# A selective scan's products partly a chunk earlier, and a layer norm pass in written order

## The chip, the core and the metric

The kernel runs on one core of one Trainium2 chip. The metric is the device time of one execution in microseconds (us). A profiled execution was also taken; its trace gives the start and length of every instruction on TensorE (PE, with its weight loads PEld), VectorE (DVE), ScalarE (ACT) and GpSimd (POOL), and the waits between them. SP is the queue from which nearly all DMAs are issued.

## The reference

Two layers act on x, 256 x 256 positions with 128 channels, all in float32. Layer 0 is a group norm, a layer norm, and attention along each row with a bias from the pairs. Layer 1 is a group norm, a 3 x 3 depthwise convolution and a selective scan in four directions. What bears on the change, cut to its core:

```python
# layer 0, on the group-normed input
x = (x - mu) * rsqrt(var + EPS) * gamma + beta        # layer norm over the channels
pair_bias = x @ Wb                                    # 4 heads
...
# layer 1, for each of K = 4 directions over L = 65536 positions, 256 channels, 16 states
delta = softplus(dts + dt_bias)
def step(h, inp):
    d_t, x_t, B_t, C_t = inp
    dA = exp(d_t[..., None] * As)
    h = dA * h + (d_t * x_t)[..., None] * B_t[:, :, None, :]
    y = einsum('bkdn,bkn->bkd', h, C_t)
    return (h, y)
...                                                    # the four directions' y summed
y = (y - mu) / sqrt(var + 1e-05) * ln_w + ln_b
y = y.reshape(b, h, w, d) * z
return y @ w_out.T
```

## The kernel before

It has these stages, one after the other: the first group norm's statistics; the layer norm's pass; the attention; the convolution; the scan. The change touches the second and the last.

**The layer norm's pass** (L165 to L227) goes over 32 blocks of 2048 positions, each held as 16 slices of 128 positions by 128 channels. A block is loaded (xb, L173), GpSimd subtracts the group means (xg, L177), VectorE multiplies by the group factors, which lie in PSUM (L180), and takes each slice's mean and variance (L186, L188; into mv). GpSimd makes rs, the inverse root of the variance, by an addition and a power (L36, L37). VectorE makes nb, the mean times -rs (L192). Even slices are then normalized on VectorE with a tensor_scalar (L203), odd ones on ScalarE (L195). TensorE transposes four slices at a time into a PSUM tile tp (L216), ScalarE evacuates it into xT (L220), TensorE multiplies xT by Wb (L224), and ScalarE evacuates this into pb (L225). Both go to DRAM. The pools hold three buffers of each SBUF tile. The order of instructions on each engine is not as written there: the framework's scheduler sets it.

**The scan** (from L1042) has its order written by hand. There are 512 chunks of 512 positions: 128 for each direction, the directions one after the other. A chunk q has eight groups g of 32 channels by 16 states, laid on 128 partitions as four state quarters, and a group takes four scans, n = 0 to 3. For each of these ScalarE makes dA by an exponential (L1081; dAl in SBUF for n = 0, dA in PSUM with three buffers for the others), and VectorE scans (L1107). VectorE also makes the additive terms of three scans in one product (L838). The terms of the fourth come another way. In "products" ScalarE multiplies the transposed delta times x (duT) by B (tiles bt, L797, 16 instructions for each half of a chunk; half h has groups 4h to 4h+3, and one buffer bt for each half), and TensorE transposes a group's part back into bl (L809). GpSimd multiplies the states by C (L1127), TensorE sums these over the states (L853).

Other work of ScalarE's, TensorE's and GpSimd's is cut into pieces by generators, of which each of the 32 places of a chunk, (g, n), takes one. A list "counts" says how many products a place takes:

```python
counts = {1: [0, 2, 3, 3], 3: [2, 2, 2, 2], 5: [0, 0, 2, 2], 6: [1, 1, 2, 2], 7: [2, 2, 2, 0]}
            if g == 5 and n == 2 and q + 1 < NQ:
                multiplying.append(products(q + 1, 0))
            if g == 1 and n == 1:
                multiplying.append(products(q, 1))
```

"prepare" (L684) makes a later chunk's operands; it begins at group 5 and goes on into group 2 of the next chunk: two copies xs in group 6, the product pb in group 7, its evacuation bc (L710) at group 7, n = 2, then two Abs and two Relu, an exponential (L736), two shifts (L748, L751), and at group 2, n = 0, a logarithm (L758), which needs another table on ScalarE. "turn" (L769) transposes delta times x at group 4. When a half is summed, "evacuate" copies it (yo, L1026). At the end of a chunk of the first three directions, "store" adds the y of the direction before and writes it out. In the last direction "finish" (L910) does so and then takes the layer norm: ScalarE copies ys, VectorE takes the statistics, GpSimd makes rs and nb, ScalarE makes four yn (L952), TensorE transposes them, ScalarE makes gz (L971), GpSimd multiplies by z (L976), TensorE multiplies by w_out, and ScalarE evacuates xo (L995). The generator counts its places from group 3, n = 0, of the next chunk, and "until(now, then)" lets then - now places pass. So 16 is group 7, n = 0, and 23 is group 0, n = 3.

Of the kernel before, what the change touches and what calls it, by code (L numbers as in the profile page):

```python
# [8 lines left out]
F32 = mybir.dt.float32  # L9
# [7 lines left out]
P = 128  # L17
# [16 lines left out]
def rsqrt(nc, out, v, eps, neg_half):  # L34

    nc.gpsimd.tensor_scalar(out, v, eps, None, ALU.add)  # L36
    nc.gpsimd.tensor_tensor(out, out, neg_half.to_broadcast(list(out.shape)), ALU.pow)  # L37
# [29 lines left out]
def attention_and_scan_kernel(  # L67
# [97 lines left out]
    with tc.tile_pool(name="ln", bufs=3) as ln, tc.tile_pool(  # L165
        name="lnps", bufs=3, space=PSUM
    ) as lnps, tc.tile_pool(name="r1ps", bufs=1, space=PSUM) as r1ps:

        r1_p = r1ps.tile([P, D], F32, name="r1_p")
        nc.vector.tensor_copy(r1_p, r1)  # L170
        for b in range(S // RB):
            xb = ln.tile([P, NSL, D], F32, name="xb")
            nc.sync.dma_start(  # L173
                xb, x[b * BT : (b + 1) * BT, :].rearrange("(s p) c -> p s c", p=P)
            )
            xg = ln.tile([P, NSL, D], F32, name="xg")
            nc.gpsimd.tensor_tensor(  # L177
                xg, xb, m1.unsqueeze(1).to_broadcast([P, NSL, D]), ALU.subtract
            )
            nc.vector.tensor_tensor(  # L180
                xg, xg, r1_p.unsqueeze(1).to_broadcast([P, NSL, D]), ALU.mult
            )
            st = ln.tile([P, NSL, 6], F32, name="st")
            mv = ln.tile([P, NSL, 2], F32, name="mv")
            for s in range(NSL):
                nc.vector.bn_stats(st[:, s, :], xg[:, s, :])  # L186
            for s in range(NSL):
                nc.vector.bn_aggr(mv[:, s, :], st[:, s, :])  # L188
            rs = ln.tile([P, NSL], F32, name="rs")
            rsqrt(nc, rs, mv[:, :, 1], 1e-5, neg_half)  # L190
            nb = ln.tile([P, NSL], F32, name="nb")
            nc.vector.scalar_tensor_tensor(nb, mv[:, :, 0], -1.0, rs, ALU.mult, ALU.mult)  # L192
            for s in range(NSL):
                if s % 2:
                    nc.scalar.activation(  # L195
                        xg[:, s, :],
                        xg[:, s, :],
                        AF.Identity,
                        bias=nb[:, s : s + 1],
                        scale=rs[:, s : s + 1],  # L200
                    )
                else:
                    nc.vector.tensor_scalar(  # L203
                        xg[:, s, :],
                        xg[:, s, :],
                        mv[:, s, 0:1],
                        rs[:, s : s + 1],
                        ALU.subtract,
                        ALU.mult,
                    )  # L210
            xT = ln.tile([D, BT], F32, name="xT")
            pb = ln.tile([H, BT], F32, name="pb")
            for q in range(NSL // 4):
                tp = lnps.tile([D, 512], F32, name="tp")
                for j in range(4):
                    nc.tensor.transpose(  # L216
                        tp[:, j * P : (j + 1) * P], xg[:, 4 * q + j, :], ident
                    )
                cols = slice(q * 512, (q + 1) * 512)
                nc.scalar.activation(  # L220
                    xT[:, cols], tp, AF.Identity, bias=beta_s, scale=gamma_s
                )
                pp = lnps.tile([H, 512], F32, name="pp")
                nc.tensor.matmul(pp, wb_s, xT[:, cols], start=True, stop=True)  # L224
                nc.scalar.copy(pb[:, cols], pp)  # L225
            nc.sync.dma_start(xT_d[:, b * BT : (b + 1) * BT], xT)
            nc.sync.dma_start(pb_d[:, b * BT : (b + 1) * BT], pb)  # L227


    with tc.tile_pool(name="abias", bufs=1) as ab:  # L230
# [448 lines left out]
    def until(now, then):  # L679

        for _ in range(then - now):
            yield
# [227 lines left out]
    def finish(q, yos):  # L910

        a = steps[q][1]
        yl = summed.pop(q)
        yield
        sums_ = []
        for g in range(2):
            ps = sps.tile([P, 2, DI], F32, name="ysum", tag="mm")
            add_sum(  # L920
                ps,
                yl[:, 2 * g : 2 * g + 2, :],
                [
                    (ps[:, j, h * P : (h + 1) * P], yos[h][:, (2 * g + j) * P : (2 * g + j + 1) * P])
                    for j in range(2)
                    for h in range(2)
                ],
            )
            sums_.append(ps)
            yield  # L930
        yield
        ys = io.tile([P, 4, DI], F32, name="ys", tag="yt", bufs=1)
        for g, ps in enumerate(sums_):
            nc.scalar.copy(ys[:, 2 * g : 2 * g + 2, :], ps)
            yield
        zt = io.tile([P, 2, T], F32, name="zl", bufs=1)
        nc.sync.dma_start(zt, z_d[:, a : a + T].rearrange("(h p) t -> p h t", p=P))
        st = io.tile([P, 4, 6], F32, name="yst")
        mv = io.tile([P, 4, 2], F32, name="ymv")
        rs = io.tile([P, 4], F32, name="yrs")  # L940
        nb = io.tile([P, 4], F32, name="ynb")
        for j in range(4):
            nc.vector.bn_stats(st[:, j, :], ys[:, j, :])
        for j in range(4):
            nc.vector.bn_aggr(mv[:, j, :], st[:, j, :])
        rsqrt(nc, rs, mv[:, :, 1], 1e-5, neg_half)
        nc.gpsimd.tensor_tensor(nb, mv[:, :, 0], rs, ALU.mult)
        nc.gpsimd.tensor_scalar(nb, nb, -1.0, None, ALU.mult)
        yield from until(6, 16)
        yn = io.tile([P, 4, DI], F32, name="yn", tag="yl", bufs=1)  # L950
        for j, now, then in ((0, 16, 19), (1, 19, 20), (2, 20, 23), (3, 23, 27)):
            nc.scalar.activation(  # L952
                yn[:, j, :],
                ys[:, j, :],
                AF.Identity,
                bias=nb[:, j : j + 1],
                scale=rs[:, j : j + 1],
            )
            yield from until(now, then)
        tps = []  # L960
        for h in range(2):
            tp = sps.tile([P, T], F32, name="tpz", tag="mm")
            for j in range(4):
                nc.tensor.transpose(
                    tp[:, j * P : (j + 1) * P], yn[:, j, h * P : (h + 1) * P], ident
                )
            tps.append(tp)
        yield from until(27, 30)
        gz = io.tile([P, 2, T], F32, name="gz", bufs=1)
        for h, tp in enumerate(tps):  # L970
            nc.scalar.activation(  # L971
                gz[:, h, :], tp, AF.Identity, bias=lnb_s[:, h : h + 1], scale=lnw_s[:, h : h + 1]
            )
            yield
        yield from until(32, 36)
        nc.gpsimd.tensor_tensor(gz, gz, zt, ALU.mult)  # L976
        yield from until(36, 40)
        xr = io.tile([P, 4, D], F32, name="xr", bufs=1)
        nc.sync.dma_start(xr, x2_d[a : a + T, :].rearrange("(j p) c -> p j c", p=P))
        yield from until(40, 55)  # L980
        po = sps.tile([P, 4, D], F32, name="po", tag="mm")
        nc.tensor.matmul(po, ident, xr, start=True, stop=True)
        for j in range(4):
            for h in range(2):
                nc.tensor.matmul(
                    po[:, j, :],
                    gz[:, h, j * P : (j + 1) * P],
                    wout_s[:, h, :],
                    start=False,
                    stop=True,  # L990
                    skip_group_check=True,
                )
        yield from until(55, 58)
        xo = io.tile([P, 4, D], F32, name="xo", tag="xr", bufs=1)
        nc.scalar.copy(xo, po)  # L995
        nc.sync.dma_start(out[a : a + T, :].rearrange("(j p) c -> p j c", p=P), xo)
# [60 lines left out]
    begin_sums(0, 0)  # L1057
    turning, multiplying, summing = [], [], []
    bls = {(0, 0): turn_back(0, 0)}

    counts = {1: [0, 2, 3, 3], 3: [2, 2, 2, 2], 5: [0, 0, 2, 2], 6: [1, 1, 2, 2], 7: [2, 2, 2, 0]}
    for s, (q, g) in enumerate(all_steps):
        k, a = steps[q]
        nxt = all_steps[s + 1] if s + 1 < len(all_steps) else None
# [11 lines left out]
        for n, i in enumerate((NB, *range(NB))):  # L1076
# [18 lines left out]
                turning.append(turn(q + 1))  # L1095
            if g == 5 and n == 2 and q + 1 < NQ:
                multiplying.append(products(q + 1, 0))
            if g == 1 and n == 1:
                multiplying.append(products(q, 1))
            if g == 5 and n == 1 and q + 2 < NQ:  # L1100
                preparing.append(prepare(q + 2))
            piece(turning)
# [90 lines left out]
```

## Time and profile before

| | |
|---|---|
| median of 3 runs | 32542.47 us (32539.59 to 32545.17) |
| profiled execution | 32538.74 us, span 32537.0 us |
| VectorE busy | 29634.3 us (91%) |
| GpSimd busy | 25719.5 us (79%) |
| ScalarE busy | 25277.6 us (78%) |
| TensorE matmuls | 24581.2 us (76%) |
| layer norm's pass | 112.9 to 615.2 us |
| scan | 5714 to 32485 us |

A profile row of a group gives line, engine, operation and tiles (written <- read), shape, count, then busy time and the mean of one in ns, then the idle time of the engine ahead of these and what ended it. A row of the waits gives who waited for whom, the total in us, how often, and the longest. A row of the timeline gives start, length, engine, line, operation, tiles, shape and count, and in brackets the idle time ahead and who ended it.

### The profile page before, as it was taken

How to read it: one execution, taken by the hardware profiler on the slowest of the kernel's cores; microseconds unless marked ns; L12 is line 12 of the kernel's file. 1: busy time of each engine (PE TensorE's matmuls, PEld its weight loads, DVE VectorE, ACT ScalarE, POOL GpSimd, SP SyncE). 2: the span in 40 equal slices, each digit the busy share in tenths (PEclk: the TensorE clock that was granted, in tenths of full speed). 3: DMA queues.
4: the chain of work that ended last, by engine and by line, in shares of the span. 5: the costliest groups of instructions: out<-in, count | busy, mean ns of one | idle time of the engine just before them, and what ended most of it. 6: DMA issues, size and time to landing. Idle time of an engine off the chain costs nothing.

```text
span 32537.0 us, 380541 instructions
## 1 busy us (share of the span) xinstructions
PE 24581.2 (76%) x122902; PEld 11561.7 (36%) x122902; DVE 29634.3 (91%) x28991; ACT 25277.6 (78%) x50438; POOL 25719.5 (79%) x11291
## 2 busy tenths in 40 slices
PE   5999989777777777777777777777777777777777
PEld 2555544223222223333333333333333333333333
DVE  7666643999999999999999999999999999999999
ACT  4555522888888888888888888888888888888887
POOL 3222200899999999999999999999999999999998
PEclk8999999777777777777777777777777777777777
DMA  3001023444444444444444444444444455554554
GB/s 137 29 28 30 28 93 123 110 108 109 110 109 108 108 109 119 118 118 119 120 120 118 117 119 121 119 119 118 120 120 118 118 123 123 122 121 121 122 122 112
DMA packets 2100469, 3518.55 MB, mean 108 GB/s; under 512 B 201112, under 2 KB 1187096, under 8 KB 2022560
## 3 DMA queue, kind: packets, MB, share of 16 engines
q1 hardware_dynamic: 2093296, 3476.09, 42.8%
q8 instruction: 967, 15.84, 0.2%
q10 hardware_dynamic: 5168, 18.12, 0.1%
q14 instruction: 1038, 8.50, 0.1%
HBM read 2754.18 MB, written 739.25 MB: 107 GB/s over the span
## 4 chain that ended last, share of the span: by engine, by line
DVE 31%; PE 27%; ACT 26%; issue 10%; POOL 5%; DMA 1%; DVEq 0%; SPq 0%; POOLq 0%; ACTq 0%
DVE bx L1107 17%; DVE bx L838 9%; PE yp L853 7%; ACT dA L1081 6%; PE ur L827 5%; ACT bt L797 4%; POOL bx L1127 2%; ACT dAl L1081 2%; PE pc L526 2%; ACT L758 2%; ACT L1081 2%; PE av L356 2%; POOL at L333 2%; ACT du L751 2%; PE atp L345 2%
## 5 line engine op out<-in xcount | busy, mean ns | idle before, releaser
L1127 POOL TENSOR_TENSOR bx<-bx,C_r 128x2048 f32<-128x2048 f32 x4096 | 18604.5, 4542 | 334.5 <-POOL hst L1126 6.0
L1107 DVE TENSOR_TENSOR_SCAN bx<-dA,hst,bx 128x512 f32<-128x512 f32 x12192 | 15061.1, 1262 | 455.3 <-ACT dA L1081 455.3
L1081 ACT ACTIVATE dA<-dr,A_s 128x512 f32<-128x512 f32 x12288 | 8345.5, 684 | 2974.6 <-DVE bx L1107 2865.2
L827 PE MATMUL ur<-du,spread 128*128 128x512 f32 x8192 | 5998.0, 823 | 4593.9 <-DVE bx L838 4544.3
L838 DVE TENSOR_TENSOR bx<-B_r,ur 128x1536 f32<-128x1536 f32 x4096 | 7067.5, 1725 | 39.1 <-DMA dr<-de_d 39.1
L797 ACT ACTIVATE bt<-duT,B_t 128x128 f32<-128x128 f32 x16384 | 5625.5, 394 | 0.0
L1107 DVE TENSOR_TENSOR_SCAN bx<-dAl,hst,bl 128x512 f32<-128x512 f32 x4064 | 5091.9, 1253 | 5.3 <-PE bl L809 4.3
L853 PE MATMUL yp<-bx,gather 128*32 128x512 f32 x32768 | 4808.1, 739 | 7.4 <-POOL bx L1127 6.4
L809 PE MATMUL bl<-ident,bt 128*128 128x128 f32 x16384 | 2817.3, 297 | 2060.9 <-DVE bx L1107 2049.9
L827 PEld LDWEIGHTS ur<-du,spread 128*128 128x128 f32 x8192 | 1519.7, 232 | 5194.1 <-DVE bx L838 5178.5
L809 PEld LDWEIGHTS bl<-ident,bt 128*128 128x128 f32 x16384 | 1871.7, 148 | 3949.2 <-DVE bx L1107 2874.1
L333 POOL TENSOR_TENSOR at<-at,sm 128x2048 f32<-128x2048 f32 x256 | 922.3, 3603 | 2708.9 <-DVE sm L332 2595.6
L1081 ACT ACTIVATE dAl<-dr,A_s 128x512 f32<-128x512 f32 x4096 | 2915.1, 712 | 0.0
L853 PEld LDWEIGHTS yp<-bx,gather 128*32 128x32 f32 x32768 | 1110.2, 134 | 4153.9 <-issue 4018.1
L1126 POOL COPY hst<-bx 128x4 f32<-128x4 f32 x4096 | 773.6, 189 | 1830.0 <-DVE bx L1107 1800.0
L325 ACT ACTIVATE at<-at,mx 128x256 f32<-128x256 f32 x2048 | 1016.1, 498 | 472.3 <-DVE mx L321 467.9
L755 POOL TENSOR_TENSOR e<-e,du 128x1024 f32<-128x1024 f32 x512 | 1206.6, 2357 | 137.7 <-DMA C_r<-bc_d 137.7
L766 POOL TENSOR_TENSOR du<-delta,xs 128x1024 f32<-128x1024 f32 x512 | 1208.9, 2361 | 40.2
L762 POOL TENSOR_TENSOR delta<-delta,lg 128x1024 f32<-128x1024 f32 x512 | 1208.8, 2361 | 40.2
L721 PE MATMUL pv<-bc,dtw_s 8*128 8x512 f32 x2048 | 1014.3, 614 | 256.8 <-ACT bc L710 256.8
L760 POOL TENSOR_TENSOR lg<-lg,e 128x1024 f32<-128x1024 f32 x512 | 1204.9, 2353 | 0.2 <-ACT lg L758 0.2
L354 DVE COPY aT<-atp 128x512 f32<-128x512 f32 x512 | 353.5, 690 | 772.8 <-PE atp L345 772.8
(172 smaller groups left out, 33209.5 us busy)
## 6 DMA issues: line engine op xcount, KB each, us to landing
dr<-de_d SPq DMA_DIRECT2D x4096, 256.0 KB
C_r<-bc_d SPq DMA_DIRECT2D x2048, 256.0 KB
B_r<-bc_d SPq DMA_DIRECT2D x2048, 192.0 KB
de_d<-delta SPq DMA_DIRECT2D x512, 512.0 KB
xtok<-xc_d SPq DMA_DIRECT2D x256, 512.0 KB
xtok<-xc_d SPq DMA_DIRECT2D x512, 256.0 KB
yl<-y_d SPq DMA_DIRECT2D x512, 256.0 KB
y_d<-yt SPq DMA_DIRECT2D x512, 256.0 KB
```

Of the source, the lines that this page charges most:

```text
L333: nc.gpsimd.tensor_tensor(at, at, sm.unsqueeze(3).to_broadcast([P, H, 2, S]), ALU.mult,)
L755: nc.gpsimd.tensor_tensor(e, e, du, ALU.subtract)
L762: nc.gpsimd.tensor_tensor(delta, delta, lg, ALU.add)
L766: nc.gpsimd.tensor_tensor(du, delta, xs, ALU.mult)
L797: nc.scalar.mul(bt[:, b, :, j, :], duT[:, b, h * P : (h + 1) * P].rearrange("t (g c) -> t g c", c=32), B_t[:, b, n : n + 1],)
L809: nc.tensor.transpose(bl[:, b * P : (b + 1) * P], bt[:, b, g % 4].rearrange("t j c -> t (j c)"), ident)
L827: nc.tensor.matmul(ur, spread[:, g % 4].rearrange("p j c -> p (j c)"), prepared[q][2][:, g // 4, :], start=True, stop=True,)
L838: nc.vector.tensor_tensor(bx[:, :NB, :], prepared[q][3], ur.unsqueeze(1).to_broadcast([P, NB, T]), ALU.mult,)
L853: nc.tensor.matmul(yp[32 * g : 32 * g + 32, :], gather, hc[:, i, :], start=(i == 0 and steps[q][0] != ORDER[0]), stop=True, skip_group_che ...
L1081: nc.scalar.activation(dA, dr, AF.Exp, scale=A_s[:, k, g // 4, g % 4, i : i + 1])
L1107: nc.vector.tensor_tensor_scan(hs[:, i, :], dA, hs[:, i, :] if i < NB else bls.pop((q, g)), 0.0 if a == 0 else hst[:, g, i : i + 1], ALU.mult,
L1127: nc.gpsimd.tensor_tensor(hs, hs, prepared[q][4], ALU.mult)
```

## The change

In the scan, the products of a chunk's second half are queued at group 7 of the chunk before rather than at group 1 of their own, and the counts put four of the 16 there, four in group 1 and eight in group 3. The first half's are put closer together. Ahead of the loop the first chunk's first four are made. In "finish" the four yn stand one place or more earlier and the two gz one place later.

In the layer norm's pass the order is written by hand. Loads run two blocks ahead, the subtraction one block ahead, and a block is normalized after the statistics and rsqrt of the next one have been issued. The means are copied to a PSUM tile mp, from which nb reads them. The product with Wb and its evacuation come one group of four slices behind the transposes.

```diff
+        def token_stats(xg):
...
+            mp = r1ps.tile([P, NSL], F32, name="mp", bufs=2)
+            nc.vector.tensor_copy(mp, mv[:, :, 0])
+            return mv, mp
+
+        def normalize(b, xg, mv, mp, rs):
...
-            nc.vector.scalar_tensor_tensor(nb, mv[:, :, 0], -1.0, rs, ALU.mult, ALU.mult)
+            nc.vector.scalar_tensor_tensor(nb, mp, -1.0, rs, ALU.mult, ALU.mult)
...
+            for q in range(NQ0 + 1):
+                if q < NQ0:
+                    tps[q] = lnps.tile([D, 512], F32, name="tp")
...
+                if q:
+                    cols = slice((q - 1) * 512, q * 512)
+                    pp = lnps.tile([H, 512], F32, name="pp", bufs=2)
+                    nc.tensor.matmul(pp, wb_s, xT[:, cols], start=True, stop=True)
+                    nc.scalar.copy(pb[:, cols], pp)
...
+        with tc.manual_schedule():
+            xbs = {b: load_block(b) for b in range(2)}
+            xg = center(xbs.pop(0))
+            before = None
+            for b in range(NB0):
+                if b + 2 < NB0:
+                    xbs[b + 2] = load_block(b + 2)
+                nxt_xg = center(xbs.pop(b + 1)) if b + 1 < NB0 else None
+                mv, mp = token_stats(xg)
+                rs = ln.tile([P, NSL], F32, name="rs")
+                rsqrt(nc, rs, mv[:, :, 1], 1e-5, neg_half)
+                if before is not None:
+                    normalize(*before)
+                before = (b, xg, mv, mp, rs)
+                xg = nxt_xg
+            normalize(*before)
...
-        yield from until(6, 16)
+        yield from until(6, 15)
...
-        for j, now, then in ((0, 16, 19), (1, 19, 20), (2, 20, 23), (3, 23, 27)):
+        for j, now, then in ((0, 15, 16), (1, 16, 19), (2, 19, 20), (3, 20, 27)):
...
-        yield from until(27, 30)
+        yield from until(27, 31)
...
-        yield from until(32, 36)
+        yield from until(33, 36)
...
+    multiplying.append(products(0, 1))
+    for _ in range(4):
+        piece(multiplying)
+
+
-    counts = {1: [0, 2, 3, 3], 3: [2, 2, 2, 2], 5: [0, 0, 2, 2], 6: [1, 1, 2, 2], 7: [2, 2, 2, 0]}
+    counts = {1: [0, 0, 2, 2], 3: [2, 2, 2, 2], 5: [0, 0, 3, 3], 6: [2, 2, 2, 2], 7: [2, 2, 2, 0]}
...
-            if g == 1 and n == 1:
-                multiplying.append(products(q, 1))
+            if g == 7 and n == 1 and q + 1 < NQ:
+                multiplying.append(products(q + 1, 1))
```

## The prediction

> **What bounds the kernel now.** I read the page first, for the engine that is full, then the waits of that engine by stretch, then the timeline around its wait, and last the layer norm's pass.
>
> ```profile
> PE 24581.2 (76%) x122902; PEld 11561.7 (36%) x122902; DVE 29634.3 (91%) x28991; ACT 25277.6 (78%) x50438; POOL 25719.5 (79%) x11291
> L1107 DVE TENSOR_TENSOR_SCAN bx<-dA,hst,bx 128x512 f32<-128x512 f32 x12192 | 15061.1, 1262 | 455.3 <-ACT dA L1081 455.3
> ```
>
> The scan of the second layer runs from 5714 to 32485 us, and there VectorE is full. Its only idle time of size stands ahead of the scans that read dA: 455 us. The waits by stretch (first three scan directions from 5714, 12350 and 19000 us, the last from 25550) give 71.7, 71.0 and 68.5 us, then this:
>
> ```profile
> DVE bx L1107 <- ACT dA L1081: 248.9, 126, 2.2
> ```
>
> About one wait per chunk of 512 tokens (128 chunks a direction): 0.55 us in the first three directions, 1.95 us in the last. The timeline of one chunk of the last direction shows its place, ScalarE first:
>
> ```profile
> 29098.26 0.58 ACT L710 COPY bc<-pb 40x512 f32<-40x512 f32 x1 [0.82 <-PE pb L704]
> 29101.06 0.59 ACT L952 ACTIVATE yn<-ys,ynb,yrs 128x256 f32<-128x256 f32 x1
> ...
> 29105.66 0.61 ACT L952 ACTIVATE yn<-ys,ynb,yrs 128x256 f32<-128x256 f32 x1
> 29106.15 1.06 ACT L736 ACTIVATE e<-e 128x1024 f32<-128x1024 f32 x1
> ...
> 29112.17 1.01 ACT L797 ACTIVATE bt<-duT,B_t 128x128 f32<-128x128 f32 x3
> 29113.05 0.70 ACT L1081 ACTIVATE dA<-dr,A_s 128x512 f32<-128x512 f32 x1
> 29113.66 1.00 ACT L797 ACTIVATE bt<-duT,B_t 128x128 f32<-128x128 f32 x3
> 29114.54 0.74 ACT L1081 ACTIVATE dAl<-dr,A_s 128x512 f32<-128x512 f32 x1
> 29115.30 1.28 ACT L758 ACT_TABLE_LOAD   x1
> 29116.59 1.06 ACT L758 ACTIVATE lg<-lg 128x1024 f32<-128x1024 f32 x1
> 29117.67 1.28 ACT L1081 ACT_TABLE_LOAD   x1
> 29118.96 1.30 ACT L1081 ACTIVATE dA<-dr,A_s 128x512 f32<-128x512 f32 x2
> ```
>
> and VectorE in the same chunk:
>
> ```profile
> 29116.44 1.25 DVE L1107 TENSOR_TENSOR_SCAN bx<-dAl,hst,bl 128x512 f32<-128x512 f32 x1
> 29119.69 1.28 DVE L1107 TENSOR_TENSOR_SCAN bx<-dA,hst,bx 128x512 f32<-128x512 f32 x1 [1.99 <-ACT dA L1081]
> ```
>
> From bc (group 7) to the second exponential of group 2, ScalarE works without a gap. The chain ends in the logarithm with a table load on either side (3.66 us), and VectorE waits for the exponential behind it. The chain's start is no choice of ScalarE's: at bc it waited 0.82 us for TensorE's pb, which follows VectorE's own products. So what lies between bc and that exponential is paid in full; what lies before bc, up to its idle time, is free.
>
> The layer norm's pass, 112.9 to 615.2 us, is 15.7 us for each of 32 blocks. VectorE's groups in it, and two places of its timeline:
>
> ```profile
> L192 DVE SCALAR_TENSOR_TENSOR nb<-mv,rs 128x16 f32<-128x16 f32 x32 | 112.7, 3521 | 86.3 <-POOL rs L37 86.3
> L62 DVE COPY gn_r_row<-gn_rstd 128x128 f32<-128x128 f32 x1 | 4.5, 4515 | 6.0 <-POOL gn_rstd L37 6.0
> L170 DVE COPY r_p<-gn_r_row 128x128 f32<-128x128 f32 x1 | 0.3, 295 | 0.0
> 312.71 2.13 DVE L203 TENSOR_SCALAR xg<-xg,mv,rs 128x128 f32<-128x128 f32 x8
> 181.60 6.43 DVE L203 TENSOR_SCALAR xg<-xg,mv,rs 128x128 f32<-128x128 f32 x8
> ```
>
> nb has 16 columns and takes 3.5 us, as GpSimd's subtraction (L177, 4.49 us) stands beside it; alone it takes 0.17 us. The last two lines are the same eight instructions, without and with that subtraction beside them (it starts at 182.16 us).
>
> **The scan, part by part.** Of the 16 products of the second half (bt, 16 per chunk), 8 stood in group 1 ahead of the logarithm; now 4 do, and 4 move to group 7 of the chunk before. To make room, the first half's 16 go from 2,2 / 1,1,2,2 / 2,2,2 to 3,3 / 2,2,2,2 / 2,2 over groups 5, 6 and 7. Group 7 keeps 2,2,2. No instruction is added, but for four products of the first chunk (1.2 us, once).
>
> *Taken from the chain:* 4 products. In the chunk shown three products and the next exponential start 29112.17 and 29113.05, so 0.29 us each: 1.18 us.
>
> *Put elsewhere:* 2 more in group 5, 2 more in group 6's first half. In the last direction ScalarE there waits for VectorE by 3.2 us and 1.8 us before two exponentials, in the others 1.6 and 1.8 us, so 0.6 us in each place is hidden; the cover goes only with these waits, and then the chunk loses up to 1.2 us.
>
> *An added wait:* the early products overwrite bt of the same half, so ScalarE at group 7 waits until TensorE has transposed it (L809) for group 7; behind it stand an exponential, yo and bc. In a chunk of the first direction those transposes ran 9003.53 to 9004.19, where the two products of that place started at 9003.62: 0.6 us, against 0.49 us of idle time before the next exponential and 0.92 us before bc. Hidden; in the last direction the extra yn already brings ScalarE there later than the transposes.
>
> *The finish's moves* (last direction): the four yn (0.49 us from start to start) shift one place up, so two of them rather than three lie behind bc: 0.49 us off the chain. One more lies before bc, in its 0.82 us. gz goes half a group later, behind the wait, where exponentials are over 1.6 us ahead. GpSimd's product and the later DMAs keep their places; SP's loads keep their order.
>
> *Sum.* Last direction: wait 1.99 us, plus 0.07 us which the scan after a wait loses of its overlap (group 2 takes 8.42 us rather than 6.36), less 1.18 + 0.49 = 1.67: 0.39 us is left. 128 x 1.67 = 214 us. Other directions: group 2 takes 7.02 us on the mean and would take 6.36; in four chunks of five the wait is 0.38 us and goes wholly, in the fifth bc comes late by 1 us or more and some 0.4 us stays in half of these. 384 x 0.62 = 238 us. Together 452 us. What is late next: GpSimd. Around one chunk of the last direction it is idle for only 1.05 + 1.55 us of 54.6, and 1.67 us of that goes; it still catches up once a chunk.
>
> **The layer norm.** Program order puts the statistics of block b before the normalizing of b-1 and rsqrt before the next subtraction. Added: 32 copies of the means into PSUM. The trace has none, but L170 (SBUF to PSUM, 128 columns) took 0.3 us beside a subtraction and L62 (SBUF to SBUF) 4.5 us; I take 0.15 us, between 0.1 and 0.3, so 5 us. nb falls from 3.52 to 0.17 us.
>
> By the nb row alone the gain is 32 x 3.35 = 107 us. [...]
> - rsqrt blocks: 4.5 + 3.3 + 0.5 + 4.6 to 5.8, so 12.9 to 14.1 us a block, and the gain is 32 x (15.7 - these), 51 to 90 us.
> - rsqrt does not block: 9.6 to 10.8 us, gain 157 to 195 us.
>
> Its nearest row is the subtraction, which blocks, so I take the first case, 60 us, low in it as each wait between engines in the loop adds something; the second case bounds it from the other side. SP's loads run two blocks ahead and the stores of b-1 stand between them; a load behind a store that waits for ScalarE's last pb is for a subtraction a block later, and 2 MB in 14 us are 150 GB/s, where the pass's first 250 us moved 222. [...]
>
> **Total.** 452 + 60 = 512 us. The profiled execution took 32538.7 us (span 32537.0), 3.7 under the median 32542.5 of the runs shown: so 32030.
>
> **Rivals.**
> - *Layer norm free of the block*: the scan's 452 plus 170 us: 31920. For: nothing shows rsqrt blocking. Against: the subtraction does. 0.15.
> - *The scan gets half*: ScalarE's chain starts later with the earlier products and yn (bc's margin is 0.3 us in the last direction), or GpSimd, nearly full, holds the sums, and the wait is halved: 226 + 60: 32256. Against: every transfer has a wait to lie in. 0.12.
> - *Slower*: the early products stand behind TensorE's transposes of bl, which in group 6 follow 32 matmuls of the sums. If those end over 0.8 us later than in the trace, bc moves; beyond 0.8 + 1.2 us the chain is longer than before. At 3 us late each of 512 chunks loses 1 us, which leaves 32542 + 512 - 60 = 32994. Against: the sums end where they did. 0.04.
> - *The change does nothing*, as the wait was set elsewhere: the exponential ends 0.03 us before the scan starts, which excludes it nearly. 0.02.
>
> **How the numbers follow.** The forecast has 0.67 with its own range 31980 to 32110. With the free layer norm and the half scan the range is 31910 to 32250; outside lie the slow cases, a part of the half scan and a little of the free layer norm. Faster by over 0.2% (65 us, about what a measurement here can tell): 0.94. Within: 0.02. Slower: 0.04.
>
> **What would show it.** DVE waits for dA near 20 us in the first three directions together and 40 us in the last; 51.0 us a chunk, then 52.9 (before 51.5 and 54.6). nb at 0.2 us, and L203's successor with a mean well above the 0.401 us of before and maxima near 4.5 us; tensor_scalars at 0.33 throughout would speak for the first rival. If bc no longer waits for pb, or VectorE waits for dA in another group, the scan's ledger is wrong.

## The result, and the profile after

| | before | after |
|---|---|---|
| median, on the same chip | 32543.82 us (4 runs, 32539.59 to 32546.18) | 32184.13 us (4 runs, 32180.22 to 32187.91) |
| ratio | | 0.989 (95% interval 0.9872 to 0.9907) |
| span of the profiled execution | 32537.0 us | 32185.1 us |
| mean granted TensorE clock | 0.818 | 0.853 |
| layer norm's pass ends at | 615.2 us | about 485 us |
| scan starts at | 5714 us | 5590 us |

The kernel gained 360 us where 512 were forecast. The layer norm's pass gave 130 us, the scan the other 230. The forecast had 60 and 452: the first was half of what came, the second twice.

From the page of the profile after, the engines and the scan's row (busy us, mean ns, idle time before and what ended it):

```profile
PE 23853.4 (74%) x122902; PEld 10868.3 (34%) x122902; DVE 29575.2 (92%) x29023; ACT 25201.0 (78%) x50438; POOL 25710.4 (80%) x11291
L1148 DVE TENSOR_TENSOR_SCAN bx<-dA,hst,bx 128x512 f32<-128x512 f32 x12192 | 15074.4, 1264 | 217.2 <-ACT dA L1122 215.3
```

VectorE's idle time before the scans that read dA fell from 455 to 217 us, not to the 60 that the forecast named. In the last direction (the waits from 25500 us) it is

```profile
DVE bx L1148 <- ACT dA L1122: 144.2, 122, 1.9
```

still a wait in nearly every one of 128 chunks, 1.2 us each on the mean. The wait is in the same place (group 2, its second exponential).

In the layer norm's pass (VectorE's groups, 100 to 620 us) nb is free, as forecast, and the tensor_scalar took over what held it:

```profile
L215 DVE TENSOR_SCALAR xg<-xg,mv,rs 128x128 f32<-128x128 f32 x256 | 134.9, 595 | 0.0
L199 DVE COPY mp<-mv 128x16 f32<-128x16 f32 x32 | 5.7, 178 | 1.1
L204 DVE SCALAR_TENSOR_TENSOR nb<-mp,rs 128x16 f32<-128x16 f32 x32 | 5.3, 165 | 1.1 <-POOL rs L37 1.1
```

One block shows which of GpSimd's instructions holds it. These are VectorE's rows, GpSimd's, and the spread (shortest, median, longest, in ns) of the eight tensor_scalars of that block:

```profile
307.58 0.17 DVE L204 SCALAR_TENSOR_TENSOR nb<-mp,rs 128x16 f32<-128x16 f32 x1
307.66 4.17 DVE L215 TENSOR_SCALAR xg<-xg,mv,rs 128x128 f32<-128x128 f32 x8
305.44 4.51 POOL L183 TENSOR_TENSOR xg<-xb,gn_m_row 128x2048 f32<-128x2048 f32 x1 [3.12 <-DVE st L195]
310.25 2.92 POOL L37 TENSOR_TENSOR rs<-rs,neg_half 128x16 f32<-128x16 f32 x1
L215 DVE TENSOR_SCALAR xg<-xg,mv,rs x8: 331/332/2370, 307.7 to 311.5; 128x128 f32<-128x128 f32 x8
```

The subtraction runs until 309.95 us. The first tensor_scalar begins beside it and ends with it (2.37 us). The other seven go by at 0.33 us, and the last five of them start while the power (L37, from 310.25 us) is running. Counted over the pass, 30 of the 256 tensor_scalars stand beside a subtraction and take 1.0 to 4.5 us; 218 overlap a power and take 0.33 to 0.35 us. The power is not held either: it takes 2.92 to 2.93 us in both traces, though before none of the tensor_scalars stood beside it.

A subtraction now starts every 10.87 us, where it was 15.29. In 25 of 29 blocks it starts 0.14 us behind the last transposes of three blocks earlier, which free its buffer.

**What TensorE did ahead of bc.** The sum for the scan rested on bc starting where it did. So look at TensorE in the eighth group of one chunk of the first direction. Before (group 7's first scan, dAl, starts at 8954.48 us):

```profile
8945.89 1.52 PE L827 MATMUL ur<-du,spread 128*128 128x512 f32 x2 [2.16 <-DVE bx L838]
8947.35 4.88 PE L853 MATMUL yp<-bx,gather 128*32 128x512 f32 x32
8952.16 0.66 PE L809 MATMUL bl<-ident,bt 128*128 128x128 f32 x4
8952.66 1.02 PE L827 MATMUL ur<-du,spread 128*128 128x512 f32 x2
8953.61 1.91 PE L704 MATMUL pb<-xs,xw_in 128*40 128x512 f32 x4
```

After (that scan starts at 8706.72 us):

```profile
8698.12 2.07 PE L864 MATMUL ur<-du,spread 128*128 128x512 f32 x2 [2.16 <-DVE bx L875]
8700.12 5.52 PE L890 MATMUL yp<-bx,gather 128*32 128x512 f32 x32
8705.58 0.66 PE L846 MATMUL bl<-ident,bt 128*128 128x128 f32 x4
8706.07 1.02 PE L864 MATMUL ur<-du,spread 128*128 128x512 f32 x2
8707.02 1.91 PE L741 MATMUL pb<-xs,xw_in 128*40 128x512 f32 x4
```

The instructions are the same, and TensorE starts them after the same wait: over the chunks of the first and last directions ur starts 8.6 us ahead of that scan in the median, in both kernels. But from the start of ur to that of bl it takes 7.46 us, not 6.27. Against the scan, bl starts 1.14 us ahead of it rather than 2.32, and pb 0.30 us behind it rather than 0.87 ahead. The rows by stretch, from ur to bl, before and then after, give the cause in their PEclk (the third number from the end, the clock's share of full speed):

```profile
8945.89:8952.16 6.27, 6.27 (x34) 1.38 (x35) 6.27 (x6) 5.09 (x12) 6.19 (x3) 0.73 0.00 0
```

```profile
8698.12:8705.58 7.46, 7.46 (x35) 1.74 (x35) 7.46 (x7) 5.55 (x14) 7.38 (x3) 0.61 0.00 0
```

TensorE runs these matmuls at 0.61 of its clock rather than 0.73, in a kernel whose mean clock went up. ScalarE's rows of the same chunk after show what came of it:

```profile
8706.27 0.69 ACT L834 ACTIVATE bt<-duT,B_t 128x128 f32<-128x128 f32 x2 [1.72 <-PE bl L846]
8706.87 0.67 ACT L1122 ACTIVATE dA<-dr,A_s 128x512 f32<-128x512 f32 x1
8707.48 0.57 ACT L1063 COPY yo<-yp 128x512 f32<-128x512 f32 x1
8708.97 0.58 ACT L747 COPY bc<-pb 40x512 f32<-40x512 f32 x1 [0.91 <-PE pb L741]
```

The products wait 1.72 us for bl (the wait that the change added), and then bc waits another 0.91 us for pb. So bc starts 2.25 us behind the scan; in the chunk before it was 1.08.

The books of the chain, medians over the chunks of the trace (the first number for the first three directions, the chain's from the first alone; the second for the last direction):

| us | before | after |
|---|---|---|
| bc starts after group 7's first scan | 1.06; 0.97 | 2.25; 2.17 |
| from bc to the end of group 2's second exponential | 19.61; 21.39 | 18.25; 19.73 |
| sum | 20.67; 22.36 | 20.50; 21.90 |
| chunk | 51.37; 54.61 | 51.20; 54.16 |
| chunk, mean | 51.54; 54.57 | 51.18; 53.85 |

The chain was cut by 1.36 and 1.66 us. bc came 1.2 us later. The median chunk got what was left: 0.17 and 0.45 us. The total follows from the means, in which the chunks that came off the median count too: 384 x 0.36 + 128 x 0.72 = 230 us.

The last direction of the kernel after shows the link by itself, since TensorE's clock ahead of bc differs there from chunk to chunk. These are medians over the chunks of four bands:

| bc after the scan | chunks | clock from ur to bl | ur to bl | group 2 of the next chunk |
|---|---|---|---|---|
| 0.82 to 0.88 us | 26 | 0.75 | 6.07 us | 6.75 us |
| 1.70 to 1.75 us | 23 | 0.65 | 6.94 us | 7.63 us |
| 2.16 to 2.19 us | 23 | 0.61 | 7.38 us | 8.07 us |
| 2.31 to 2.41 us | 24 | 0.60 | 7.60 us | 8.29 us |

The instructions are the same in all of them and ur starts in the same place. By as much as bc is later, group 2 is longer. In the first band the next chunk takes 52.85 us, which is what the forecast had (52.9). In 19 more chunks bc came at 2.44 to 2.52 us; VectorE then loses part of its time earlier, in waits for bl.

### The profile page after: what moved, and what is told of

It reads as the page before. It is cut to its first block, busy times and chain, and to the rows that moved or that the text cites. A ratio compares the mean times of both kernels' runs of the same rounds, so it can differ in the third digit from the quotient of the medians.

```text
span 32185.1 us, 380702 instructions
## 1 busy us (share of the span) xinstructions
PE 23853.4 (74%) x122902; PEld 10868.3 (34%) x122902; DVE 29575.2 (92%) x29023; ACT 25201.0 (78%) x50438; POOL 25710.4 (80%) x11291
## 4 chain that ended last, share of the span: by engine, by line
PE 32%; ACT 24%; DVE 22%; issue 12%; POOL 9%; DMA 2%; SPq 0%; ACTq 0%; POOLq 0%; DVEq 0%
DVE bx L1148 11%; PE yp L890 8%; DVE bx L875 7%; ACT dA L1122 6%; PE ur L864 6%; POOL bx L1168 5%; PE pb L741 3%; ACT bt L834 2%; PE pc L563 2%; ACT dAl L1122 2%; PE av L393 2%; PE tpy L913 2%; POOL at L370 2%; ACT e L765 2%; ACT L795 2%
## 5 line engine op out<-in xcount | busy, mean ns | idle before, releaser
L864 PE MATMUL ur<-du,spread 128*128 128x512 f32 x8192 | 5710.1, 787 | 4498.5 <-DVE bx L875 4378.8
L890 PE MATMUL yp<-bx,gather 128*32 128x512 f32 x32768 | 5052.5, 771 | 7.5 <-POOL bx L1168 6.4
L846 PE MATMUL bl<-ident,bt 128*128 128x128 f32 x16384 | 2714.8, 289 | 2441.0 <-DVE bx L1148 2439.0
L846 PEld LDWEIGHTS bl<-ident,bt 128*128 128x128 f32 x16384 | 1791.0, 143 | 4323.4 <-DVE bx L1148 3240.7
L864 PEld LDWEIGHTS ur<-du,spread 128*128 128x128 f32 x8192 | 1451.2, 223 | 5027.9 <-DVE bx L875 5023.9
```

Source lines behind the costliest of these rows:

```text
L846: nc.tensor.transpose(bl[:, b * P : (b + 1) * P], bt[:, b, g % 4].rearrange("t j c -> t (j c)"), ident)
L864: nc.tensor.matmul(ur, spread[:, g % 4].rearrange("p j c -> p (j c)"), prepared[q][2][:, g // 4, :], start=True, stop=True,)
L890: nc.tensor.matmul(yp[32 * g : 32 * g + 32, :], gather, hc[:, i, :], start=(i == 0 and steps[q][0] != ORDER[0]), stop=True, skip_group_che ...
```

## Experiments

**One part alone.** norm_alone is the kernel after with the scan of before; scan_alone is the kernel before with the scan of after. Of each edit a few lines (the others are those of the change's diff, taken back or taken over):

```diff
# norm_alone, on after
-        for j, now, then in ((0, 15, 16), (1, 16, 19), (2, 19, 20), (3, 20, 27)):
+        for j, now, then in ((0, 16, 19), (1, 19, 20), (2, 20, 23), (3, 23, 27)):
...
# scan_alone, on before
-            if g == 1 and n == 1:
-                multiplying.append(products(q, 1))
+            if g == 7 and n == 1 and q + 1 < NQ:
+                multiplying.append(products(q + 1, 1))
```

> The layer norm's pass of the changed kernel with the scan of before. Both theories of the scan: the pass ends 130 us earlier (485 rather than 615 us in the two traces) and the scan keeps its 51.5 us a chunk and 54.6 in the last direction, so 32543 - 130 = 32413 us. If instead the pass's gain depends on what follows, or the attention gives some of it back, 32450 or more.

Measured: 32413.71 us, ratio 0.9962 (0.9947 to 0.9977), 126 us less than before on that chip.

> The scan of the changed kernel with the layer norm's pass of before. If the parts add up: 32543 - 228 = 32315 us, with 51.2 us a chunk in the first three directions and 53.8 in the last. If the phase at which the scan starts decides (theory: TensorE's clock comes in windows of 3.41 us, and the chunk locks to 15 of them), the first three directions still give 51.20 us a chunk, and only the last may differ by some tens of us.

Measured: 32319.61 us, ratio 0.9933 (0.9917 to 0.995), 220 us less. The parts add up to 346 us against the 360 of both together. In scan_alone the scan starts 123 us later than in after, and its chunks of the first three directions take 51.20 us again.

**The added wait.** The early four products get a tile of their own with two buffers, so that they wait for no transpose:

```diff
-        bt = wk.tile([P, 4, 4, 4, 32], F32, name=f"bt{h}", bufs=1)
+        if h:
+            first = wk.tile([P, 4, 4, 32], F32, name="bt1a", bufs=2)
+            rest = wk.tile([P, 3, 4, 4, 32], F32, name="bt1b", bufs=1)
+            bt = [first, *(rest[:, b] for b in range(3))]
...
```

> The changed kernel, where the four early products have a second buffer, so that they no longer wait for TensorE's transposes of group 7. Theory A (these products' wait on ScalarE, 699 us in all, holds bc and the logarithm): the waits for dA go and the time falls by 150 to 220 us, to some 31990. Theory B (bc waits for pb anyway, as TensorE reaches pb 1.2 us later than before): the wait of 699 us goes, bc's wait for pb grows by as much, and the time stays within 30 us of 32184.

Measured: 32190.94 us, ratio 0.9893 (0.9879 to 0.9908): no gain on after. ScalarE's waits in the kernel after:

```profile
ACT bt L834 <- PE bl L846: 698.7, 481, 1.9
ACT bc L747 <- PE pb L741: 455.3, 512, 3.0
```

and with two buffers (bt's wait is gone):

```profile
ACT bc L747 <- PE pb L741: 964.3, 512, 3.0
DVE bx L1154 <- ACT dA L1128: 219.5, 454, 2.0
```

The wait moved from bt to bc, and VectorE's stayed: 219.5 us against 217.3. The largest new wait of the trace, 699 us, costs nothing, since pb is late too. What is late is TensorE's pb.

**TensorE's clock.** If a half clock makes TensorE late, and if the half clock follows from its idle time ahead of the sums (2.16 us in the rows above), which no run had shown yet, work in that time should help, though it adds matmuls. kept_busy is after with transposes repeated (they write the same values again): those of the second half of the states (tps) four times, those of bl for group 6 five times, 28 more transposes a chunk.

```diff
             tp = sps.tile([P, T], F32, name="tps", tag="mm")
-            for j in range(4):
-                nc.tensor.transpose(...)
+            for _ in range(1 + 3 * h):
+                for j in range(4):
+                    nc.tensor.transpose(...)
...
-        for b in range(4):
-            nc.tensor.transpose(bl...)
+        for _ in range(5 if g == 6 else 1):
+            for b in range(4):
+                nc.tensor.transpose(bl...)
```

> The changed kernel with TensorE kept busy in group 5: 12 transposes of tps and 16 of bl are done again with the same outputs, in the two idle stretches (1.5 and 2.2 us) ahead of the sums. Theory B (TensorE comes to the sums at half its clock, so these end 1.2 us late and with them bl, ur, pb and bc): full clock at the sums, bc 1.2 us earlier, no lock to 51.20 us: 50.9 us a chunk and 52.9 in the last direction, 32184 - 210 = 31975 us. Theory A, or a TensorE that is late for want of time and not of clock: no gain, or slower by the 2 us of added work a chunk (up to 600 us).

Measured: 32014.17 us, ratio 0.9839 (0.9824 to 0.9853), 170 us less than after (166 by the ratios, as the two ran on different chips). Its row for the stretch from ur to bl in the chunk shown above, and VectorE's wait in the whole trace:

```profile
8677.22:8681.85 4.63, 4.63 (x35) 1.24 (x35) 4.63 (x5) 3.76 (x11) 4.55 (x3) 1.00 0.01 4
```

```profile
DVE bx L1150 <- ACT dA L1124: 26.4, 125, 1.7
```

At full clock (1.00 in this stretch, where after has 0.61) the same matmuls take 4.63 us instead of 7.46. bc starts 0.76 to 0.92 us behind the scan in all chunks but one (1.03). The wait is 26 us, and a chunk of the first direction takes 50.89 us, which is eight groups of 6.36 us: VectorE without a gap. In the last direction the chain is as long as in after (19.73 us); only its start moved (0.77 us behind the scan rather than 2.17).

The same repeats in the kernel before ask how much of this belongs to the change:

> The kernel before with TensorE kept busy in group 5, by the same repeated transposes as in e4. Theory B: what the clock cost before was the fifth of the chunks in which bc came 1 us or more late (group 2 takes 7.02 us on the mean and 6.84 in the others): 384 x 0.17 = 65 us, so 32475; the wait of 0.38 us and of 1.99 us in the last direction stay, since they are ScalarE's work. If keeping TensorE busy is worth 170 us by itself, whatever the products' place, 32370.

Measured: 32458.75 us, ratio 0.9972 (0.9961 to 0.9983), 87 us less, nearer to the 65 expected than to the 170: by the mean chunk the first three directions gave 58 us and the last 24, which the 65 had not counted. The chain, whose work is left as it was, now starts at 0.77 us in the median of all four directions, and what it costs stays: group 2 takes 6.85 us in the first three directions and 8.29 in the last. Between this kernel and kept_busy lie 445 us (433 by the ratios), of which some 130 are the layer norm's. So with these repeats in both kernels the scan's changes are worth 300 to 315 us, where they gave 230 without.

busy_twice is kept_busy with the transposes of bl for group 3 repeated too.

```diff
-        for _ in range(5 if g == 6 else 1):
+        for _ in range(5 if g in (3, 6) else 1):
```

> The changed kernel with TensorE kept busy in group 5 as in e4, and ahead of group 3's sums too (16 more transposes of bl, in an idle stretch of up to 4.3 us). In e4 what is left are waits for bl at group 4 (0.14, 0.11 and 0.40 us a chunk in directions two to four) and 0.19 us for dA in the last. Theory B: these are the half clock at group 3; they go, and the time falls by 30 to 90 us from 32014, to some 31950. If they are work and not clock, the same or slower.

Measured: 31945.60 us, ratio 0.9815 (0.98 to 0.9829). It is the fastest of all these kernels, 600 us under before. Against kept_busy, VectorE's waits for bl fell from 93.3 to 33.2 us. In the row by stretch VectorE (the third busy time) fills the first direction without a gap, GpSimd (the fifth) does not:

```profile
5800.00:12000.00 6200.00, 4862.59 (x23875) 2490.03 (x23874) 6200.00 (x4875) 5304.01 (x10236) 5721.32 (x2438) 0.84 0.46 110
```

**The forecast's two terms, with the clock held.** old_finish is kept_busy with finish's old places, old_products is kept_busy with the products where they stood before. Each undoes one term of the sum.

```diff
# old_finish
-        for j, now, then in ((0, 15, 16), (1, 16, 19), (2, 19, 20), (3, 20, 27)):
+        for j, now, then in ((0, 16, 19), (1, 19, 20), (2, 20, 23), (3, 23, 27)):
...
# old_products
...
-    counts = {1: [0, 0, 2, 2], 3: [2, 2, 2, 2], 5: [0, 0, 3, 3], 6: [2, 2, 2, 2], 7: [2, 2, 2, 0]}
+    counts = {1: [0, 2, 3, 3], 3: [2, 2, 2, 2], 5: [0, 0, 2, 2], 6: [1, 1, 2, 2], 7: [2, 2, 2, 0]}
-            if g == 7 and n == 1 and q + 1 < NQ:
-                multiplying.append(products(q + 1, 1))
+            if g == 1 and n == 1:
+                multiplying.append(products(q, 1))
```

> The kernel kept_busy with the products of the second half where they stood before (none a chunk ahead, 8 of them in group 1 ahead of the logarithm) and the finish's new places. The ledger (four products, 1.18 us of chain in every chunk): before_kept_busy, which has the old products too, showed 6.86 us for group 2 against 6.36 without a wait in the first three directions, so 384 x 0.5 = 192 us there, and up to 1.18 us in the last, 128 x 1.18 = 151 us, less the wait that is left there now: about 32014 + 300 = 32310, between 32270 and 32360. If the products' place matters little once TensorE is not late: 32014 to 32100.

Measured: 32265.22 us, ratio 0.9914 (0.9898 to 0.9931), 251 us slower than kept_busy (244 by the ratios). Group 2 takes 6.85 us in the first three directions, as expected, and in the last 7.80 us against 6.65: 1.15 us for the four products, where the sum had 1.18. The total is below the 300 expected, and just outside the range given with it, as kept_busy itself still loses time in group 3 of the second to fourth directions (6.48 to 6.80 us, against 6.36 to 6.39 in old_products).

> The kernel kept_busy (after, with TensorE transposing the second half of the states four times and group 6's bl five times, which took 32014 us at a wait for dA of 0.19 us a chunk in the last direction) with the finish's old places: one yn more lies behind bc again. The ledger (0.49 us of chain for one yn, in the 128 chunks of the last direction alone): 63 us slower, 32077, and the last direction's median chunk 0.4 to 0.5 us longer than 52.77 us. If the place of yn has no price once bc is early: 32014 within 15 us.

Measured: 32021.05 us, ratio 0.984 (0.9825 to 0.9854), only 7 us slower than kept_busy (3 by the ratios). The two scan rows, kept_busy's first:

```profile
L1150 DVE TENSOR_TENSOR_SCAN bx<-dA,hst,bx 128x512 f32<-128x512 f32 x12192 | 15219.2, 1282 | 24.7 <-ACT dA L1124 24.7
```

```profile
L1150 DVE TENSOR_TENSOR_SCAN bx<-dA,hst,bx 128x512 f32<-128x512 f32 x12192 | 15219.5, 1282 | 86.0 <-ACT dA L1124 86.0
```

The yn has its price on the chain: 61 us more of waiting, and a median chunk of 53.26 us against 52.77, 0.48 where 0.49 was expected. But VectorE's wait for bl in the last direction falls from 49 to 6 us at the same time, so the sum hardly shows it. The term was right on the chain and the total of 63 us was missed. Why the waits for bl fell was not looked into.

**The layer norm.** means_from_sbuf is after with nb reading mv in SBUF and without the copy; means_alone is before with only that copy added and read by nb.

```diff
# means_from_sbuf, on after
-            nc.vector.scalar_tensor_tensor(nb, mp, -1.0, rs, ALU.mult, ALU.mult)
+            nc.vector.scalar_tensor_tensor(nb, mv[:, :, 0], -1.0, rs, ALU.mult, ALU.mult)
...
# means_alone, on before
+            mp = r1ps.tile([P, NSL], F32, name="mp")
+            nc.vector.tensor_copy(mp, mv[:, :, 0])
-            nc.vector.scalar_tensor_tensor(nb, mv[:, :, 0], -1.0, rs, ALU.mult, ALU.mult)
+            nc.vector.scalar_tensor_tensor(nb, mp, -1.0, rs, ALU.mult, ALU.mult)
```

> The kernel before with one edit: nb reads the means from a PSUM copy; the order is still the scheduler's. Theory D: nb falls from 3.5 to 0.17 us and the time by 107 us, to some 32433. Theory C: the tensor_scalars take over the block and the time stays within 25 us of 32540.

Measured: 32507.65 us, ratio 0.9988 (0.9981 to 0.9995), 38 us less than before: between the two expectations and nearer to that of the lock passed on. Its groups in the pass:

```profile
L205 DVE TENSOR_SCALAR xg<-xg,mv,rs 128x128 f32<-128x128 f32 x256 | 175.3, 749 | 30.0 <-POOL rs L37 30.0
L194 DVE SCALAR_TENSOR_TENSOR nb<-mp,rs 128x16 f32<-128x16 f32 x32 | 5.3, 167 | 17.9 <-POOL rs L37 17.9
```

nb lost 107 us of busy time (112.7 to 5.3), and the tensor_scalars took on 90 of them (85.1 to 175.3): the next instruction in line inherits most of the subtraction's block.

> The changed kernel where nb reads the means from SBUF, as before, in the new order. In the changed kernel's trace the subtraction stands beside nb in 30 of 32 blocks, and the first tensor_scalar behind nb takes 1.0 to 4.5 us instead of 0.33. Theory C (whoever is first in line is blocked): nb takes the block in the tensor_scalar's place, and the time stays within 40 us of 32184. Theory D (the nb row is the gain): 30 blocks times up to 4.3 us come back, up to 32300.

Measured: 32226.83 us, ratio 0.9901 (0.9886 to 0.9916), 43 us slower than after (36 by the ratios), at the edge of the first expectation. nb takes 1.78 us on the mean here, and the tensor_scalars 587 ns, nearly what they take in after. The block alternates: in 15 of the 32 blocks nb takes 1.5 to 4.3 us and all eight tensor_scalars are short, in 15 others nb is short and one tensor_scalar takes 4.5 to 4.7 us. Whoever stands there is held. The scan starts at 5626 us, 88 before the kernel before and 36 behind the kernel after. So of the pass's 130 us the written order gives some 90 and the means in PSUM some 40. By itself the means' place gave 38 us in the old order too.

## Why the prediction was right, and where not

- *The place and the chain's sum: right.* The wait stayed where it was named. The chain from bc on was cut by 1.66 us in the last direction, where the sum had 1.18 + 0.49 = 1.67. Undone one at a time at a held clock, the terms measured 1.15 and 0.48.
- *"In the others 0.62 us a chunk": the chain's part right, the result not.* The chain fell by 1.36 us, more than the 1.18 counted. The chunk gained 0.17 us in the median and 0.36 in the mean, which counts the chunks in which bc came late before.
- *"Hidden", and "the sums end where they did": this step failed.* The working set 0.6 us of waiting against 0.49 and 0.92 us of idle time, with bl and pb at their places of before. They are not fixed: bl and pb came 1.2 us later against VectorE. The added wait is not the reason (two buffers changed nothing); TensorE's clock is (0.61 rather than 0.73 from ur to bl, and the wait was 26 us with it held at full). For a TensorE that is not late the sum was right, as the kernel after itself shows: behind an early bc the last direction's chunk took 52.85 us, and the 32 chunks of the second and third directions behind a bc at 2.0 us or less took 50.89 in the median, where the forecast had 52.9 and 51.0. busy_twice ends there too (50.9 and 52.9 on the mean). Its scan gains some 470 us on before, but not from the change alone: the repeats for group 6 gave 87 us on the kernel before.
- *"What is late next: GpSimd": wrong.* TensorE was, by its clock. In busy_twice VectorE is full for most of the first direction (6200 us) while GpSimd still has idle time (5721 of 6200 us busy).
- *The rival that gets half of the scan* named 226 us, close to the 230 measured, but for causes that the runs exclude: the chain's start moved by TensorE, neither by ScalarE's products and yn nor by GpSimd. The slower rival had the right place (sums that end late hold bl, then bc) and set the point at 0.8 us: they ended 1.2 us late, which is short of its 0.8 + 1.2 us, beyond which the chain would be longer than before, so the change still gained. It named no cause that could make them late; the clock was one.
- *The layer norm: that the lock passes on was rightly preferred to the nb row, but one instruction too many was counted as a lock.* Before, eight tensor_scalars took 6.43 us with a subtraction beside them and 2.13 without. After, the lock passed from nb to them, as forecast: a mean of 595 ns, 30 of 32 blocks with one of 1.0 to 4.5 us. "rsqrt blocks", the 3.3 us on which the 60 us rest, failed: no run shows a power that holds a tensor_scalar, and here 218 of 256 ran at 0.33 to 0.35 us beside one. The sum without that term was right: a subtraction every 10.87 us, against 9.6 to 10.8 us. Its other terms behind the subtraction, 0.5 and 4.6 to 5.8 us, no run shows by themselves; in their place the trace after has 6.36 us on the mean from the end of a subtraction to the start of the next (10.87 less 4.51), which in 25 of 29 blocks comes 0.14 us behind the last transposes of three blocks earlier. Its gain of 157 to 195 us was still too high, as it set the loop against 15.7 us, which is the whole pass divided by 32; the loop before took 15.29. So it gave 31 x 4.42 = 137 us, and the time from the start of the last subtraction to the end of the pass grew from 28 to 35 us, which leaves 130. That the loads would keep up was right, though the 222 GB/s named for it is of the kernel's first 250 us, of which 112 lie ahead of the pass; from 118 to 468 us the new pass moved 182.

## What to carry to other kernels

A sum over one engine's chain holds only if its gate comes on time: before a chain's start is called fixed, read the granted clock of the engine that gates it (here TensorE's, 0.61 where it was 0.73), and look where that engine idles. A large new wait may cost nothing and a small old one may decide, so take the new one away before blaming it. Where a clock or a start differs from chunk to chunk in one trace, sort the chunks by it: that is an experiment already run. A loop's time is to be set against the old loop's, not against a stage divided by its blocks. When an instruction is freed from a lock, look at what stands next in line (in means_alone nb lost 107 us, and the tensor_scalars took on 90), and check in the trace which partners really lock (in the kernel after the subtraction did, in 30 of 32 blocks; the power, beside 218 tensor_scalars, did not).

## What the runs showed of the hardware

**A loop that locks to TensorE's clock.** The traces' clock records have it at 1.0 or 0.5 only (1592 records of each in the kernel after), in stretches that are multiples of 3.413 us, but for the last, which ends with the trace. The starts of all 3184 stretches, and of the 3674 in the kernel before, lie on one grid of that step to within 0.06 us. A step of the grid is called a window here. In the kernel after, chunks of the first direction take 51.192 to 51.224 us from the fifth on, which is 15 windows (15 x 3.4133 = 51.20), and bc starts 2.25 or 2.26 us behind its scan in over 100 chunks running; that scan starts 2.69 to 2.77 us into a window in all of them. The kernel before drifts: 51.37 us is 0.17 us over 15 windows. So in ten chunks (515.42 us, 151 windows) it goes once past a whole window. The first direction repeats this: eight chunks with bc at 0.84 to 1.07 us, whose scans start from 0.99 to 2.16 us into a window, 0.17 us later each time, then one at 2.47 (2.33 us into a window) and one at 1.78 (0.30 us). The last direction before took 54.61 us a chunk, which is 16 windows, with its scan 1.93 us into a window and bc at 0.97 us. The last direction after is not locked: behind its first chunks they take 52.8 to 54.7 us, and bc goes through 0.83, 1.72, 2.17 and 2.40 us and back, with its scan 2.23, 0.42, 2.93 and 2.47 us into a window. So in both traces bc's start goes with the scan's place in the window, with a jump near 2.2 us (before, 0.85 us at 2.16 and 2.47 us at 2.33). kept_busy, whose clock is 1.00 from ur to bl, has no such lock and takes 50.89 us. Why a chunk settles on a whole number of windows is not shown: the lock was not tried apart, for instance with a chunk made longer by a known amount.

**Idle work that pays.** 28 repeated transposes a chunk gained some 170 us on after and 87 on before; 16 more gained some 70 us more on after.

**A power beside tensor_scalars.** GpSimd's power on 128 x 16 (2.92 us) left VectorE's tensor_scalars at 0.33 us and was not itself longer for them; its subtraction on 128 x 2048 (4.5 us) held 30 of them until it ended. Whether the operation or the size makes the difference was not tried.
